# Attention values product in 64x32 array tiles instead of 32x32, with the weight quarters swapped by six SBUF transfers per block

## The chip, the cores and the metric

The kernel runs on one core of one Trainium2 chip. The metric is the device time of one execution in microseconds (us), the median of several runs. Five engines work beside each other: PE (TensorE, with PEld for its weight loads), DVE (VectorE), ACT (ScalarE), POOL (GpSimd) and SP (SyncE). Here SP computes nothing: it issues nearly all the transfers (DMAs), one after the other, in the order of the program, and when one of them must wait, all the later ones wait behind it.

## What is computed

A cross attention block with adaptive layer norm, all in 32-bit floats. The parts that matter:

```python
xq  = _ada_ln(x_q, t_vec, Wss_q, bss_q)        # x_q: (16, 1024, 512)
xkv = _ada_ln(x_kv, t_vec, Wss_kv, bss_kv)     # x_kv: (16, 64, 512)
q  = (xq @ Wq + bq).reshape(B, Lq, 16, 32)
kv = (xkv @ Wkv + bkv).reshape(B, 64, 2, 16, 32)
k, v = kv[:, :, 0], kv[:, :, 1]
scores = jnp.einsum('bqhd,bkhd->bhqk', q, k) / jnp.sqrt(32.0)
attn = jax.nn.softmax(scores, axis=-1)
out = jnp.einsum('bhqk,bkhd->bqhd', attn, v).reshape(B, Lq, 512)
return x_q + (out @ Wp + bp)
```

There are 16 heads of 32 features, and 64 keys to a batch.

## The kernel before

The 16 x 1024 query rows are cut into 32 blocks of 512 rows, numbered i; two blocks share the keys and values of one batch. The 512 features are 4 chunks c of 128, and each chunk holds 4 heads r. The 64 keys are 2 halves z of 32 keys.

The schedule is written out by hand: the order of the calls in the program is the order on every engine's queue. Blocks 0 to 2 are interleaved with the start (weights, keys, values), the loop over `i` from 3 to 29 (line 1404) has one block of each stage in flight, and the last two blocks are again written out. In one turn of the loop, block i is scored, block a = i-1 is mixed with the values, blocks b = i-2 and a are projected, block n = i+1 gets its queries, and the features of block f = i+2 are scaled.

The stages that the change and the prediction touch:

- `score_products` (651): for each half z, 16 matmuls with 32x32 tiles. The scores of head (c, r) lie on partitions 32c to 32c+31 (the 32 keys of the half) in column group r. So `s_tiles[i, z]`, 128 partitions x 4 heads x 512 queries, has the four chunks above one another and one half of the keys.
- `subtract` (715, POOL) takes the maxima `mb` off; `weights` (721, ACT) takes the exponential in place; `total` (753, POOL) adds the two halves; `row_total` (760, DVE) sums it over the keys.
- `inverse_rows` (774): DVE takes the reciprocal `lt`, and SP sends it to DRAM (`ltd`, one transfer) and back in another layout (`vr`, four transfers that wait until `ltd` has landed).
- `mix` (810): for each half z, chunk c and head r one matmul of a 32x32 tile over 512 queries: 32 in all, the second half added to the first in PSUM. `v_tiles` come from `V_all`, with the keys of a half on 32 partitions for each chunk.
- `value_move` (626): the values, computed with 128 keys of two batches on the partitions (`stages`), are moved into `V_all` by 8 transfers a call, in runs of 512 bytes; there are two calls for each of the two groups of batches, all near the start.
- `move` (381): the features of block i+3 change their layout by 16 transfers of 64 KB from SBUF to SBUF (`xt<-ht`); `scale_features` (444, ACT) waits for all 16 one turn later.
- `load_x` (106) loads 1 MB for block i+5; `load_residual` (122) loads 1 MB for block i into the buffer from which block b was just written out (`added`, 964, two transfers of 512 KB).

SP's order in one turn of the loop is: the two outputs, `load_residual`, `load_x`, `ltd`, four `vr`, sixteen `xt<-ht`. ACT's order around the weights is: first half's exponential (1435), `query_out`, `scale_features` of two chunks (1437), second half's exponential (1446).

Of the kernel before, what the change touches and what calls it, by code (L numbers as in the profile page):

```python
# [9 lines left out]
F32 = mybir.dt.float32  # L10
AF = mybir.ActivationFunctionType
ALU = mybir.AluOpType
# [3 lines left out]
P = 128  # L16
# [4 lines left out]
def cross_attention_block(  # L21
# [18 lines left out]
    nc = tc.nc  # L40
# [298 lines left out]
    def hidden(i, ts):  # L339

        for t in ts:
            row, rstd = x_tiles[i][:, t, :], q_rstd[i]
            if i == "A" and t % 2 == 0:
                nc.vector.tensor_scalar(
                    row, row, rstd[:, 0, t : t + 1], rstd[:, 1, t : t + 1], ALU.mult, ALU.add
                )
            else:
                normalise(row, row, rstd, t)
# [95 lines left out]
    def scale_features(i, cs=range(NC)):  # L444
        xt, b = xt_tiles[i], i // BPB
        for c in cs:
            nc.scalar.activation(  # L447
                xt[:, :, c, :],
                xt[:, :, c, :],
                AF.Identity,  # L450
                scale=ss["q"][:, c, b : b + 1],
                bias=ss["q"][:, NC + c, b : b + 1],
            )
# [25 lines left out]
    def feature_sums(i, eng=nc.gpsimd, steps=range(4)):  # L479

        if i in GROUPS:
            if i not in xsums:
                pool, tag = (big, "big1") if i == "A" else (opool, "ot")
                xsums[i] = pool.tile([P, 4, HC, HT], F32, tag=tag, name=f"xk_sums_{i}")
        else:
            if "q" not in xsums:
                xsums["q"] = qpool.tile([P, 4, 2, HC, P], F32, tag="wq", name="xt_sums")
            xsums[i] = xsums["q"]
        t = xsums[i]
        b12 = feature_half(i, 0, 1)  # L490
        for k in steps:
            dst, a, b = (
                (t[:, 0], feature_half(i, 1, 1), b12),
                (b12, b12, feature_half(i, 0, 0)),
                (t[:, 1], feature_half(i, 1, 1), b12),
                (t[:, 2], feature_half(i, 1, 0), t[:, 1]),
            )[k]
            eng.tensor_tensor(dst, a, b, ALU.subtract)  # L498
# [57 lines left out]
    def query_product(i, n):  # L556
        seven(i, "q", n, (0, 1))
# [27 lines left out]
            nc.vector.tensor_tensor(dst, src, dst, ALU.add)  # L585

    K_all = {g: kvpool.tile([P, NC, TB], F32, tag=f"K{g}", name=f"K_{g}") for g in GROUPS}
    V_all = {g: kvpool.tile([P, PER, 2, P], F32, tag=f"V{g}", name=f"V_{g}") for g in GROUPS}
    for g, at in GROUPS.items():
        for bl in range(PER):  # L590
            k_tiles[at * PER + bl] = K_all[g][:, :, bl * LKV : (bl + 1) * LKV]
            v_tiles[at * PER + bl] = V_all[g][:, bl]

    def key_out(i, n):
        k, m, h = OUTS[n]
# [12 lines left out]

    def value_places(i, m, h, k):
        if i not in stages:  # L610
            stages[i] = wpool.tile([P, NT, H], F32, tag="WT", name=f"stage_{i}")
        dst = stages[i][:, 2 * h : 2 * h + 2, m * HO : (m + 1) * HO]
        return qa["v", k].rearrange("p (t f) -> p t f", t=2), dst

    def value_out(i, n):
        k, m, h = OUTS[n]
        src, dst = value_places(i, m, h, k)
        b = b_v_sb[:, m * HO : (m + 1) * HO]
        nc.vector.tensor_tensor(dst, src, b.unsqueeze(1).to_broadcast([P, 2, HO]), ALU.add)

    def value_added(i, n):
        k, m, h = ADDS[n]
# [1 line left out]
        nc.vector.tensor_tensor(dst, src, dst, ALU.add)  # L624

    def value_move(i, m):
        for c in (2 * m, 2 * m + 1):
            for j in range(2):
                for z in range(2):
                    at = j * LKV + z * HK  # L630
                    nc.sync.dma_start(  # L631
                        V_all[i][32 * c : 32 * c + 32, j::2, z, :],
                        stages[i][at : at + HK, :, c * P : (c + 1) * P],
                    )

    def context_product(i, name, n):
        seven(i, name, n, CONTEXT_BANKS[i, name])
# [80 lines left out]

    l_tiles = {}

    def weights(i, z):
        p = s_tiles[i, z]
        nc.scalar.activation(p, p, AF.Exp, scale=SCALE)  # L723

    def sums(i, z):
        if z == 0:
            l_tiles[i] = small.tile([P, 2, HPC, NJ], F32, tag="l2", name=f"l2_{i}", bufs=1)
        nc.vector.tensor_reduce(
            l_tiles[i][:, z],
            s_tiles[i, z].rearrange("p r (j a) -> p r j a", a=32),  # L730
            AX.X,
            ALU.add,
            apply_transpose=True,
        )
# [18 lines left out]
    def total(i):  # L753

        pool, tag = (xpool, "x") if i == NB - 2 else (big, f"big{(i + 1) % 2 * 2}")
        t = pool.tile([P, HPC, TB], F32, tag=tag, name=f"sum_{i}")
        nc.gpsimd.tensor_tensor(t, s_tiles[i, 0], s_tiles[i, 1], ALU.add)  # L757
        sum_tiles[i] = t

    def row_total(i):  # L760
# [49 lines left out]
    def mix(i, apart=True, ks=(None,) * NC):  # L810

        vt = v_tiles[i // BPB]

        if apart:
            pairs = [ps_s.tile([P, 2, TB], F32, tag="s", name=f"po_{i}_{e}") for e in range(2)]
            po = [pairs[c // 2][:, c % 2, :] for c in range(NC)]
            po_tiles[i] = pairs
        else:
            po = [bank(f"po_{i}_{c}", ks[c]) for c in range(NC)]
            po_tiles[i] = po  # L820
        for z in range(2):
            p = s_tiles.pop((i, z))
            for c in range(NC):
                rows = slice(32 * c, 32 * c + 32)
                for r in range(HPC):
                    nc.tensor.matmul(  # L826
                        po[c][32 * r : 32 * r + 32, :],
                        lhsT=vt[rows, z, 32 * r : 32 * r + 32],
                        rhs=p[rows, r, :],
                        start=(z == 0),  # L830
                        stop=(z == 1),
                    )

    def mixed(i, es=(0, 1)):
# [389 lines left out]
    weights(0, 0)  # L1224
    turn(3, (0,))
    weights(0, 1)
    scale_features(2, (1,))
    total(0)
    hidden(3, (2,))
    q_stats(4, (2,))  # L1230
    query_product(1, 5)
# [61 lines left out]
    scale_features(3, (2,))  # L1293
    turn(4, (0,))
    weights(1, 1)
    feature_sums(2, nc.gpsimd, (3,))
    query_product(2, 7)
    query_product(2, 5)
# [6 lines left out]
    project_seeded(0, 0)  # L1305
    turn(4, (2,))
    total(1)
    query_added(2, 5)
    projected(0, 0)
    query_product(2, 4)  # L1310
# [57 lines left out]
    row_sums(1, 0)  # L1368
    turn(5, (0,))
    weights(2, 1)  # L1370
    scale_features(4, (1,))
    turn(5, (1,))
    added(1, 1)
# [6 lines left out]
    product(1, 2)  # L1380
    added(1, 2)
    total(2)
    query_product(3, 4)
    turn(5, (3,))
    biased(1, 3)
# [18 lines left out]
    for i in range(3, NB - 2):  # L1404
        a, b, n, f = i - 1, i - 2, i + 1, i + 2

        scores(i, 0, crossed=True)
        product(b, 6)
        added(b, 6)
        query_product(n, 1)  # L1410
        query_seed(n)
        added(b, 7)
        scores(i, 1)
        product(b, 5)
        added(b, 5)
        maxima(i)
        subtract(i)
        product(b, 4)
        if i < NB - 3:
            hidden(i + 3, (0, 1, 2))  # L1420
        query_product(n, 2)
        query_out(n, 2)
        product(b, 3)
        spread_rows(a)
        if i < NB - 3:
            hidden(i + 3, (3,))
        added(b, 4)
        added(b, 3)
        biased(a, 2)
        load_residual(i)  # L1430
        mix(a)
        divided(a)
        row_sums(a, 0)
        query_product(n, 6)
        weights(i, 0)
        query_out(n, 6)
        scale_features(f, (0, 1))
        product(a, 1)
        if i + 4 < NB:
            q_stats(i + 4, (0,))  # L1440
        added(a, 1)
        product(a, 2)
        if i + 4 < NB:
            q_stats(i + 4, (1,))
        added(a, 2)
        weights(i, 1)
        total(i)
        query_product(n, 7)
        query_out(n, 7)
        biased(a, 3)  # L1450
        scale_features(f, (2, 3))
        row_sums(a, 1)
        if i < NB - 3:
            turn(i + 3, range(NT))
        if i < NB - 5:
            load_x(i + 5)
        elif i == NB - 3:
            load_residual(NB - 1)
        query_product(n, 5)
        query_added(n, 5)  # L1460
        if i + 4 < NB:
            q_stats(i + 4, (2,))
        query_product(n, 4)
        query_added(n, 4)
        if i + 4 < NB:
            q_stats(i + 4, (3,))
        query_product(n, 3)
        query_out(n, 3)
        feature_sums(f)
        product(a, 7)  # L1470
        row_total(i)
        inverse_rows(i)
        if i + 3 < NB:
            move(i + 3)
        if i + 4 < NB:
            q_scale(i + 4)
# [28 lines left out]
    query_product(z, 3)  # L1505
    query_out(z, 3)
    weights(y, 1)
    total(y)
    product(y - 2, 3)
    added(y - 2, 3)  # L1510
    load_residual(y)
# [22 lines left out]
    product(y, 1)  # L1534
    added(y, 1)
    weights(z, 1)
    product(y, 2)
    added(y, 2)
    biased(z, 3)
# [73 lines left out]
```

## Time and profile before

| | |
|---|---|
| three runs | 1031.79, 1030.08, 1030.09 us (median 1030.09) |
| profiled execution | 1030.86 us, of which 1029.1 us are the span of the profile |
| PE busy | 1009.3 us of the span |
| POOL, DVE, ACT busy | 805.9, 860.9, 638.6 us |
| DMA | 149.82 MB, mean 146 GB/s; the engines' queue of SP 45.3% of the span |
| 500 to 529 us, one turn of the loop | PE busy 29.00 us of 29.00, granted clock 1.00, DMA share 0.47 |

"Busy" is the time in which an engine had an instruction running. A turn of the loop takes 29.1 us. The transfers that SP issues are not busy time of an engine; they are seen in SP's timeline (when each was issued) and in the share of the DMA engines.

### The profile page before, as it was taken

What the parts mean: (1) busy time and instruction counts of PE and PEld (TensorE: products, weight loads), DVE (VectorE), ACT (ScalarE), POOL (GpSimd) and SP (SyncE); (2) the same over time, 40 slices, a digit from 0 to 9 for tenths busy, and PEclk for the clock granted to TensorE, in tenths of its full rate; (3) what the DMA queues carried; (4) which work ended last, traced back from release to release, by engine and by line L of the source; (5) the groups of instructions that cost most, each with busy time, mean ns of one, the idle gap of its engine ahead of it and who ended that gap; (6) DMA issues with size and microseconds to landing.
All of it is one profiled execution on the core that took longest, in us unless ns stands there. A gap on an engine that the chain in (4) does not pass through costs nothing.

```text
span 1029.1 us, 21212 instructions
## 1 busy us (share of the span) xinstructions
PE 1009.3 (98%) x8077; PEld 763.4 (74%) x8077; DVE 860.9 (84%) x1174; ACT 638.6 (62%) x1025; POOL 805.9 (78%) x518
## 2 busy tenths in 40 slices
PE   8999899999999999999999999999999999999998
PEld 7877556777777777777777778777777777777746
DVE  6686669889888888889898888898888888876795
ACT  3786565666666666667666666666666676665530
POOL 4566687798888888898888888988888888987861
PEclk9999999999999999999999999999999999999999
DMA  9563544444544444445444444445434444335122
GB/s 318 179 188 119 149 122 136 157 157 156 165 155 121 143 128 154 152 152 166 140 134 146 150 133 153 156 159 165 148 110 151 134 154 154 113 125 166 46 85 85
DMA packets 112197, 149.82 MB, mean 146 GB/s; under 512 B 34104, under 2 KB 45392, under 8 KB 112096
## 3 DMA queue, kind: packets, MB, share of 16 engines
q1 hardware_dynamic: 111712, 147.94, 45.3%
q8 instruction: 64, 1.05, 0.4%
q0 software_dynamic: 384, 0.54, 0.3%
q14 instruction: 37, 0.30, 0.1%
HBM read 79.21 MB, written 34.60 MB: 111 GB/s over the span
## 4 chain that ended last, share of the span: by engine, by line
PE 81%; SPq 6%; DMA 5%; DVE 4%; ACT 1%; issue 1%; POOL 1%; DVEq 0%; ACTq 0%; POOLq 0%
PE pp L955 34%; PE pq L539 33%; PE po L826 6%; PE ps L658 6%; SPq L387 4%; DMA ltd<-lt 1%; SPq L631 1%; PE pk_A L539 1%; PE pv_A L539 1%; DMA xt<-ht 1%; DMA r<-in_x_dram 1%; DVE ht L365 1%; DVE lt L762 1%; DMA wss_kv<-in_L_xcond_Wss_kv_dram 1%; DMA x<-in_x_dram 1%
## 5 line engine op out<-in xcount | busy, mean ns | idle before, releaser
L717 POOL TENSOR_TENSOR s<-s,mb 128x2048 f32<-128x2048 f32 x64 | 290.2, 4558 | 129.3 <-DVE mb L704 127.7
L684 ACT COPY s<-ps 128x1024 f32<-128x1024 f32 x128 | 129.4, 1012 | 108.1 <-DVE m L675 64.8
L675 DVE TRANSPOSE_TENSOR_REDUCE m<-ps 128x32 f32<-128x1024 f32 x128 | 150.7, 1213 | 33.6 <-PE ps L658 33.4
L955 PE MATMUL pp<-w_p_sb,ot 128*128 128x256 f32 x720 | 165.6, 379 | 0.5 <-DVE r L979 0.4
L979 DVE TENSOR_TENSOR r<-pp,r 128x512 f32<-128x512 f32 x203 | 131.8, 670 | 30.9 <-PE pp L955 24.3
L578 ACT ACTIVATE qt<-pq,bias_t 128x256 f32<-128x256 f32 x256 | 105.6, 463 | 77.2 <-PE pq L539 77.0
L955 PEld LDWEIGHTS pp<-w_p_sb,ot 128*128 128x128 f32 x720 | 136.6, 190 | 20.5 <-issue 1.6
L723 ACT ACTIVATE s<-s 128x2048 f32<-128x2048 f32 x64 | 122.3, 1911 | 43.8 <-POOL s L717 43.8
L757 POOL TENSOR_TENSOR sum<-s,s 128x2048 f32<-128x2048 f32 x31 | 140.7, 4540 | 7.0 <-ACT s L723 7.0
L955 PEld LDWEIGHTS pp<-WT,s 128*128 128x128 f32 x480 | 86.5, 189 | 57.0 <-issue 37.7
L539 PE MATMUL pq<-xt_sums,w_q_sums 128*128 128x256 f32 x512 | 123.3, 385 | 0.0
L539 PE MATMUL pq<-xt,w_q_sums 128*128 128x256 f32 x512 | 121.1, 379 | 1.6 <-DVE qt L585 1.6
L539 PE MATMUL pq<-xt,w_q_sb 128*128 128x256 f32 x512 | 121.6, 380 | 0.3 <-ACT pq L551 0.2
L539 PEld LDWEIGHTS pq<-xt_sums,w_q_sums 128*128 128x128 f32 x512 | 94.9, 190 | 36.5 <-issue 24.8
L955 PE MATMUL pp<-WT,s 128*128 128x256 f32 x480 | 119.3, 391 | 0.2 <-POOL s L934 0.2
L955 PE MATMUL pp<-WT,ot 128*128 128x256 f32 x480 | 113.6, 379 | 0.6 <-POOL ot L931 0.6
L539 PEld LDWEIGHTS pq<-xt,w_q_sb 128*128 128x128 f32 x512 | 96.8, 190 | 16.4 <-issue 1.7
L539 PEld LDWEIGHTS pq<-xt,w_q_sums 128*128 128x128 f32 x512 | 97.2, 190 | 15.2 <-DVE qt L585 2.0
L955 PEld LDWEIGHTS pp<-WT,ot 128*128 128x128 f32 x480 | 91.0, 190 | 14.1 <-POOL ot L931 1.0
L335 ACT ACTIVATE x<-x,rstdq 128x512 f32<-128x512 f32 x128 | 97.0, 807 | 4.4 <-POOL rstdq L312 4.4
L447 ACT ACTIVATE xt<-xt,ss_q 128x512 f32<-128x512 f32 x124 | 93.9, 808 | 5.1 <-DMA xt<-ht 4.5
L498 POOL TENSOR_TENSOR xt_sums<-xt 128x512 f32<-128x512 f32 x64 | 81.4, 1272 | 14.2 <-ACT xt L447 7.3
(176 smaller groups left out, 1509.8 us busy)
## 6 DMA issues: line engine op xcount, KB each, us to landing
x<-in_x_dram SPq DMA_DIRECT2D x32, 1024.0 KB, 5.5
r<-in_x_dram SPq DMA_DIRECT2D x32, 1024.0 KB, 5.1
xt<-ht SPq DMA_DIRECT2D x488, 64.0 KB, 2.0
out_dram<-r SPq DMA_DIRECT2D x58, 512.0 KB, 3.7
out_dram<-r SPq DMA_DIRECT2D x11, 256.0 KB, 2.2
wss_kv<-in_L_xcond_Wss_kv_dram SPq DMA_DIRECT2D x4, 512.0 KB, 7.3
wss_q<-in_L_xcond_Wss_q_dram SPq DMA_DIRECT2D x4, 512.0 KB, 11.0
vr<-ltd SPq DMA_DIRECT2D x128, 8.0 KB, 1.6
```

Of the source, the lines that this page charges most:

```text
L335: nc.scalar.activation(dst, src, AF.Identity, bias=rstd[:, 1, j : j + 1], scale=rstd[:, 0, j : j + 1])
L447: nc.scalar.activation(xt[:, :, c, :], xt[:, :, c, :], AF.Identity, scale=ss["q"][:, c, b : b + 1], bias=ss["q"][:, NC + c, b : b + 1],)
L498: eng.tensor_tensor(dst, a, b, ALU.subtract)
L539: nc.tensor.matmul(out_, lhsT=lhsT, rhs=rhs, start=new and m == 0 and c == 0, stop=c == HC - 1, skip_group_check=True,)
L578: nc.scalar.activation(dst, src, AF.Identity, bias=bq_t[:, o : o + 1])
L675: nc.vector.tensor_reduce(m_tiles[i][:, z, 2 * e : 2 * e + 2, :], s_banks[i, z][e].rearrange("p r (j a) -> p r j a", a=32), AX.X, ALU.max, ...
L684: nc.scalar.copy(s_tiles[i, z][:, 2 * e : 2 * e + 2, :], s_banks[i, z][e])
L717: eng.tensor_tensor(s_tiles[i, z], s_tiles[i, z], mb_tiles[i], ALU.subtract)
L723: nc.scalar.activation(p, p, AF.Exp, scale=SCALE)
L757: nc.gpsimd.tensor_tensor(t, s_tiles[i, 0], s_tiles[i, 1], ALU.add)
L955: nc.tensor.matmul(acc[k][:, t * HO : (t + 1) * HO], lhsT=rows[:, c, t * P : (t + 1) * P], rhs=cols[:, c, :], start=n == 2 and t == 0 and ...
L979: nc.vector.tensor_add(r, a, r)
```

## The change

The product with the values works on array tiles of 64 rows and 32 columns: all 64 keys of a head lie on 64 adjacent partitions, and one matmul sums over all of them, so 16 matmuls a block stand where there were 32, and nothing is added in PSUM. For that the weights of the two halves must lie below each other. Of the four chunks, two lie right in each tile and a quarter (32 partitions, 256 KB) of each of the others is in the other tile, so quarters are swapped between the two tiles by transfers from SBUF to SBUF. The second half's exponential goes to a tile of its own (`p_`, in the buffer `spread` that the maxima `mb` also use), so that its old place can take the first half's quarters; four transfers fill that place (`paired(i, 1)`, after the exponential) and two fill the first tile (`paired(i, 0)`, called after `total`, which still reads the old contents). The values' tile gets the keys of a batch on 64 partitions, and `value_move` takes 2 transfers a call instead of 8, in runs of 4 KB.

```diff
-    V_all = {g: kvpool.tile([P, PER, 2, P], F32, tag=f"V{g}", name=f"V_{g}") for g in GROUPS}
+    V_all = {g: kvpool.tile([P, 2, 2, NT, P], F32, tag=f"V{g}", name=f"V_{g}") for g in GROUPS}
...
-            v_tiles[at * PER + bl] = V_all[g][:, bl]
+            v_tiles[at * PER + bl] = V_all[g][:, bl % 2, :, bl // 2, :]
...
     def value_move(i, m):
-        for c in (2 * m, 2 * m + 1):
-            for j in range(2):
-                for z in range(2):
-                    at = j * LKV + z * HK
-                    nc.sync.dma_start(
-                        V_all[i][32 * c : 32 * c + 32, j::2, z, :],
-                        stages[i][at : at + HK, :, c * P : (c + 1) * P],
-                    )
+        for j in range(2):
+            nc.sync.dma_start(
+                V_all[i][m * LKV : (m + 1) * LKV, j],
+                stages[i][j * LKV : (j + 1) * LKV, 2 * m : 2 * m + 2],
+            )
...
+    p_tiles = {}
+
     def weights(i, z):
-        p = s_tiles[i, z]
-        nc.scalar.activation(p, p, AF.Exp, scale=SCALE)
+        s = p = s_tiles[i, z]
+        if z == 1:
+            p = rpool.tile([P, HPC * TB], F32, tag="spread", name=f"p_{i}")
+            p = p.rearrange("p (r q) -> p r q", r=HPC)
+        nc.scalar.activation(p, s, AF.Exp, scale=SCALE)
+        p_tiles[i, z] = p
+
+    def paired(i, w):
+
+        for u in range(2):
+            first = slice(u * LKV, u * LKV + HK)
+            second = slice(u * LKV + HK, (u + 1) * LKV)
+            if w == 1:
+                nc.sync.dma_start(s_tiles[i, 1][first], p_tiles[i, 0][second])
+                nc.sync.dma_start(s_tiles[i, 1][second], p_tiles[i, 1][second])
+            else:
+                nc.sync.dma_start(s_tiles[i, 0][second], p_tiles[i, 1][first])
...
-        nc.gpsimd.tensor_tensor(t, s_tiles[i, 0], s_tiles[i, 1], ALU.add)
+        nc.gpsimd.tensor_tensor(t, p_tiles[i, 0], p_tiles[i, 1], ALU.add)
...
-        for z in range(2):
-            p = s_tiles.pop((i, z))
-            for c in range(NC):
-                rows = slice(32 * c, 32 * c + 32)
+        for w in (1, 0):
+            p = s_tiles.pop((i, w))
+            for u in range(2):
+                rows = slice(LKV * u, LKV * (u + 1))
                 for r in range(HPC):
                     nc.tensor.matmul(
-                        po[c][32 * r : 32 * r + 32, :],
-                        lhsT=vt[rows, z, 32 * r : 32 * r + 32],
+                        po[2 * u + w][32 * r : 32 * r + 32, :],
+                        lhsT=vt[rows, w, 32 * r : 32 * r + 32],
                         rhs=p[rows, r, :],
-                        start=(z == 0),
-                        stop=(z == 1),
+                        start=True,
+                        stop=True,
                     )
...
         weights(i, 1)
+        paired(i, 1)
         total(i)
+        paired(i, 0)
         query_product(n, 7)
```

The last hunk is the loop's; blocks 0 to 2, 30 and 31 get the two calls too, the last of them without `total`. On SP's queue the six transfers of the loop come behind `load_residual(i)` and before `load_x(i + 5)`. The stage of the values (`value_places`, `value_out`) is written in the new layout with the same number of instructions.

More of the change, by code (lines that the diff above doesn't have):

```diff
@@ L610, in value_places @@
         if i not in stages:
-            stages[i] = wpool.tile([P, NT, H], F32, tag="WT", name=f"stage_{i}")
-        dst = stages[i][:, 2 * h : 2 * h + 2, m * HO : (m + 1) * HO]
-        return qa["v", k].rearrange("p (t f) -> p t f", t=2), dst
+            stages[i] = wpool.tile([P, NC, NT, P], F32, tag="WT", name=f"stage_{i}")
+        dst = stages[i][:, 2 * m : 2 * m + 2, 2 * h : 2 * h + 2, :]
+        return qa["v", k].rearrange("p (t c f) -> p c t f", t=2, c=2), dst
     def value_out(i, n):
@@ L617, in value_out @@
         src, dst = value_places(i, m, h, k)
-        b = b_v_sb[:, m * HO : (m + 1) * HO]
-        nc.vector.tensor_tensor(dst, src, b.unsqueeze(1).to_broadcast([P, 2, HO]), ALU.add)
+        b = b_v_sb[:, m * HO : (m + 1) * HO].rearrange("p (c f) -> p c f", c=2)
+        nc.vector.tensor_tensor(dst, src, b.unsqueeze(2).to_broadcast([P, 2, 2, P]), ALU.add)
     def value_added(i, n):
@@ L729, in sums @@
             l_tiles[i][:, z],
-            s_tiles[i, z].rearrange("p r (j a) -> p r j a", a=32),
+            p_tiles[i, z].rearrange("p r (j a) -> p r j a", a=32),
             AX.X,
@@ L1226, in cross_attention_block @@
     weights(0, 1)
+    paired(0, 1)
     scale_features(2, (1,))
     total(0)
+    paired(0, 0)
     hidden(3, (2,))
@@ L1295, in cross_attention_block @@
     weights(1, 1)
+    paired(1, 1)
     feature_sums(2, nc.gpsimd, (3,))
@@ L1307, in cross_attention_block @@
     total(1)
+    paired(1, 0)
     query_added(2, 5)
@@ L1370, in cross_attention_block @@
     weights(2, 1)
+    paired(2, 1)
     scale_features(4, (1,))
@@ L1382, in cross_attention_block @@
     total(2)
+    paired(2, 0)
     query_product(3, 4)
@@ L1507, in cross_attention_block @@
     weights(y, 1)
+    paired(y, 1)
     total(y)
+    paired(y, 0)
     product(y - 2, 3)
@@ L1536, in cross_attention_block @@
     weights(z, 1)
+    paired(z, 1)
+    paired(z, 0)
     product(y, 2)
```

## The prediction

> **What bounds the kernel now.** I first read the page's busy times and the granted clock, then one turn of the loop on each engine's timeline (500 to 532 us), then SP's, since six transfers a block are added there. PE is busy for 98% of the span, and for all 29.00 us of the window 500 to 529 at a clock of 1.00: in the loop PE sets the pace, 29.1 us a turn.
>
> ```profile
> PE 1009.3 (98%) x8077; PEld 763.4 (74%) x8077; DVE 860.9 (84%) x1174; ACT 638.6 (62%) x1025; POOL 805.9 (78%) x518
> ```
>
> The product with the values on PE's timeline (start, length, then the group):
>
> ```profile
> 514.87 1.14 PE L658 MATMUL ps<-qt,K_A 32*32 32x512 f32 x32
> 515.94 1.99 PE L955 MATMUL pp<-WT,s 128*128 128x256 f32 x8
> ...
> 527.77 2.35 PE L826 MATMUL po<-s,V_A 32*32 32x512 f32 x64
> 530.04 1.13 PE L539 MATMUL pq<-xt_sums,w_q_sums 128*128 128x256 f32 x4
> ```
>
> From start to next start the product takes 530.04 - 527.77 = 2.27 us. A matmul of the program shows as two records, so 64 records are 32 matmuls. Taken record by record, sixteen start within 0.1 us at 527.77, the next sixteen at 528.22, then at 528.84 and at 529.29: the sixteen 32x32 tiles truly run together, in four waves of about 0.43 us (512 columns), 1.72 us, and 0.55 us go into starting, the step between the halves (528.65 to 528.84) and the end.
>
> Now SP's timeline of one turn:
>
> ```profile
> 499.56 2.49 SPq L387 DMA_DIRECT2D xt<-ht  x4
> 502.15 1.07 SPq L981 DMA_DIRECT2D out_dram<-r  x2
> 508.34 0.38 SPq L126 DMA_DIRECT2D r<-in_x_dram  x1
> 509.50 0.38 SPq L119 DMA_DIRECT2D x<-in_x_dram  x1
> 516.66 0.34 SPq L780 DMA_DIRECT2D ltd<-lt  x1
> 518.17 1.75 SPq L782 DMA_DIRECT2D vr<-ltd  x4
> 520.03 10.80 SPq L387 DMA_DIRECT2D xt<-ht  x16
> 530.92 1.07 SPq L981 DMA_DIRECT2D out_dram<-r  x2
> ```
>
> SP is one chain with few holes. It waits 508.34 - 503.22 = 5.1 us until the output has landed before the residual can be loaded into its buffer, then for the features' buffer (509.5), then 6.8 us for `lt` (516.64), then 1.2 us until `ltd` has landed, then 16 features' transfers every 0.635 us. Whatever is later than `lt` on SP makes the features later, and these have little room: the last leaves at 530.83 and, at the 2.0 us from issue to landing that the page gives for `xt<-ht`, lands at 532.3, and ACT scales them at 504.65 + 29.1 = 533.75. The room is 1.4 us. On ACT, POOL and DVE:
>
> ```profile
> 504.65 1.51 ACT L447 ACTIVATE xt<-xt,ss_q 128x512 f32<-128x512 f32 x2
> 506.63 1.91 ACT L723 ACTIVATE s<-s 128x2048 f32<-128x2048 f32 x1 [0.47 <-POOL s L717]
> ```
> ```profile
> 509.16 4.54 POOL L757 TENSOR_TENSOR sum<-s,s 128x2048 f32<-128x2048 f32 x1
> ```
> ```profile
> 513.74 2.31 DVE L762 TRANSPOSE_TENSOR_REDUCE lt<-sum 128x64 f32<-128x2048 f32 x1 [0.64 <-POOL sum L757]
> 516.09 0.55 DVE L777 RECIPROCAL lt<-lt 128x64 f32<-128x64 f32 x1
> ```
>
> Behind the scaling on ACT stand the second exponential, the next `query_out` and the seeds of PE's banks, so a late feature soon stops PE.
>
> **The matmuls.** 16 matmuls are 32 records. No 64-row tile is in the trace. Eight such tiles fill the array, so 32 records are again four waves of 512 columns: 1.72 us. What may go is part of the 0.55 us: the score product (one call of 32 records) has 515.94 - 514.87 = 1.07 us for two waves, 0.21 us over. I take 1.72 + 0.21 = 1.93, a gain of 0.34 us a block; the ends are no gain and 0.55. At 32 blocks that is 11 us, between 0 and 18, and only if PE goes on setting the pace. (The Trainium skill, TensorEngine Tiling (Array Packing), section Tiling Modes, lists 64x32 as a mode of 8 tiles; no run here shows it yet.)
>
> **The exponential, total, sums and values** keep their count and sizes, so cost nothing more. `spread` is now held by `p_` until the last swap has landed, where `mb` of the next block is written at 523.97 (its transpose on DVE); that is 15.4 us behind the exponential's end at 508.54, and the swap ends some 13 us behind it by the sum below, so it fits with 2 us. `mix` comes 19.2 us behind. `value_move` loses 24 of its 32 issues at 0.64 us, 15 us of SP's time between 62 and 134 us.
>
> **The six transfers.** Their issues are 6 x 0.62 = 3.7 us, less than SP's holes. What counts is where they stand: behind the residual's load and before `load_x`, `ltd`, `vr` and `move`, on one queue. The first four wait for the exponential (508.54), the fifth for `total` (513.70) and the first's landing, the sixth for the third's landing; `load_x` then leaves behind the sixth instead of at 509.5, and `ltd` behind both. Transfers of one queue land in order; that shows where `load_x` stands just before `ltd` already (chain of waits, 135 us): `ltd` then takes 5.16 us from its issue instead of 1.5 (516.66 to 518.17).
>
> ```profile
> 134.96 0.40 SPq L119
> 135.35 0.05 issue
> 135.41 5.16 DMA ltd<-lt
> ```
>
> The speed of a 32-partition transfer from SBUF to SBUF is read where the DMA engines are full. The windows view gives span, busy times, clock, DMA share, GB/s:
>
> ```profile
> 77.20:79.20 2.00, 2.00 (x11) 1.77 (x10) 1.97 (x2) 1.11 (x4) 0.95 (x1) 1.00 1.03 392
> 79.80:81.00 1.20, 1.20 (x7) 1.07 (x6) 0.00 (x0) 1.20 (x3) 1.20 (x1) 1.00 1.09 219
> ```
>
> The first is a load from HBM, the second mostly eight queued `xt<-ht`. So a quarter of 256 KB takes 262/219 = 1.20 us; at the load's rate it would be 0.67.
>
> The chain on SP, from `ltd` landed to the residual's issue, by the timeline: vr 1.77, to the first xt 0.1, 16 x 0.635 = 10.16, two outputs with gaps 1.1, their landing 5.1, the issue 0.4: 18.6 us. Then from that issue's end: the residual's 1 MB keep the DMA engines full until about 512.6 (share 0.96 in 510.0 to 512.5, 0.67 after), which is +3.9. The four quarters end at +5.1, 6.3, 7.5, 8.7. The third has landed at +7.8, so the sixth issue ends at +8.4, `load_x` at +8.85, `ltd` at +9.2. Quarters five and six end at +9.9 and +11.1, `load_x` (1 MB at 392 GB/s, 2.7) at +13.8, and `ltd` has landed at +14.1. The turn of this chain is 18.6 + 14.1 = 32.7 us, more than PE's 29.1: SP's queue sets the pace, 3.6 us more a turn, and PE's 0.34 us buys nothing.
>
> Sum against the profiled execution (1030.86): 24 turns (3 to 26) x 3.6 = 86. Turns 27 and 28 have no `load_x`: 32.7 - 3.1 = 29.6, 1 us in two. Blocks 0 to 2: `load_x` or the residual stood before `ltd` already, SP saves issues of values, but 7.2 us of quarters are queued in each, of which waits for loads hide most; I take +4 (-5 to 10). The end: the last exponential ends at 1000.47 and `ltd` left at 1003.75; six quarters on an idle queue (3.7 us of issues, 1.2 and 1.4 for the sixth) land at about 1008, `vr` then at 1011 instead of 1008, +3. The room of 1.4 comes off. 86 + 1 + 4 + 3 - 1.4 = 93: 1124 for an execution like the profiled one; the median of before was 0.8 lower, so **1123**.
>
> Bounds of a quarter: 0.67 us by the load's row gives landings of the third at +6.2, `load_x` issued at +7.25 and, with its own 1.3 us to the first data, done at +11.2, `ltd` +11.5: 30.1 us, 24 + 6 = 30 more, 1060. From above: the 512-byte rows of `V_B<-stage_B` took about half the rate of `xt<-ht` where the queue was full; but rows of 8 KB are nearer to the 2 KB rows. Half way, 1.6 us, gives 18.6 + 16.5 = 35.1 and 150 us more, 1180.
>
> A rule speaks against this change and yet is kinder than the row. The Trainium skill, DMA: Bandwidth & Descriptors, section Rules for kernel authors, says that transfers to separate parts of the partitions serialize, since each is spread over all 16 engines, and its Specifications give 435 GB/s as the ceiling. At that rate a quarter would be 0.60 us, the turn about 30, and an estimate from this page some 1057. The row (219 GB/s) decides.
>
> **Rivals.** (1) The swap is quick: the same chain at the load's rate, 30.1 us a turn, 1060. For it: 8 KB runs are longer than any in this trace; against: the 219 GB/s. Chance 0.20. (2) Not slower: the swap is hidden. It decides on one place, `ltd`'s landing: while that is less than 1.4 us later than now, the features are in time and PE keeps the pace. SP has 6.8 us free before `ltd`, and quarters 3.7 us of issues; if `load_x` moved 1 MB in the time before `lt`, only the matmuls' gain would be left: 1030 - 0.34 x 32 = 1019. Against it: the sixth quarter waits for the third, at about `lt`. 0.10. (3) The 64x32 tiles run one after the other: 32 x 0.43 = 13.8 us a block instead of 2.3, 368 us more, 1398. Against it: sixteen small tiles run together here. 0.03. The forecast has 0.67.
>
> **How the numbers follow.** The range 1050 to 1170 holds the forecast with most of its bounds, and rival 1. This kernel's measurement tells about 0.2% from no change. Faster is most of rival 2: 0.08; same the rest of it and a chain just at 29.1: 0.03; slower 0.89.
>
> **What would show it.** In the profile after: PE's share falls to about 90%, the chain of waits runs through SP (lines of the swap, `ltd`, `xt<-ht`, the outputs) in the loop, `ltd` takes over 4 us to land in each turn, ACT's scaling (now line 447 too) waits for `xt<-ht`, and a turn takes 32 to 33 us. The product's group would show 32 records in some 1.9 us. I am wrong if the quarters land together at over 350 GB/s, if `load_x` is not delayed to the sixth quarter, or if PE's turn stays at 29 us.

## The result, and the profile after

| | before, on the same chip | changed kernel |
|---|---|---|
| median | 1030.94 us (4 runs, 1030.08 to 1036.01) | 1202.3 us (4 runs, 1193.21 to 1204.45) |
| ratio | | 1.163 [1.156, 1.171] |
| profiled execution, its span | 1030.86, 1029.1 us | 1201.12, 1199.3 us |
| one turn of the loop, mean of blocks 3 to 26 | 29.1 us | 35.2 us |

The change costs 171 us, where 93 were forecast. The page's first part, busy time and share of the span for each engine:

```profile
PE 1049.7 (88%) x7053; PEld 779.5 (65%) x7053; DVE 866.4 (72%) x1174; ACT 637.2 (53%) x1025; POOL 805.3 (67%) x518
```

PE has 1024 records fewer than before, the 16 matmuls a block that went, and yet it is no longer the bound: 88% of a span that is 170 us longer. The product on PE's timeline of the changed kernel (start, length, group):

```profile
570.02 1.95 PE L840 MATMUL po<-s,V_A 64*32 64x512 f32 x32
571.89 1.35 PE L539 MATMUL pq<-xt_sums,w_q_sums 128*128 128x256 f32 x5
```

From start to next start it takes 571.89 - 570.02 = 1.87 us; before it took 2.27. The matmuls do what they should. The time is lost on SP. Its timeline of one turn, to be held against the one of before:

```profile
571.19 10.02 SPq L387 DMA_DIRECT2D xt<-ht  x16
581.31 1.06 SPq L995 DMA_DIRECT2D out_dram<-r  x2
585.71 0.38 SPq L126 DMA_DIRECT2D r<-in_x_dram  x1
586.18 0.51 SPq L734 DMA_DIRECT2D s<-s  x1
586.74 0.58 SPq L735 DMA_DIRECT2D s<-p  x1
587.38 0.59 SPq L734 DMA_DIRECT2D s<-s  x1
588.01 0.59 SPq L735 DMA_DIRECT2D s<-p  x1
595.27 2.62 SPq L737 DMA_DIRECT2D s<-p  x2
597.93 0.58 SPq L119 DMA_DIRECT2D x<-in_x_dram  x1
598.61 0.67 SPq L794 DMA_DIRECT2D ltd<-lt  x1
604.15 2.19 SPq L796 DMA_DIRECT2D vr<-ltd  x4
```

Four quarters go out behind the residual's load. The fifth (595.27) waits until the first has landed and the sixth until the third has; only then do `load_x` (line 119) and `ltd` (794) leave. `ltd` lands 5.5 us later, and the 16 features' transfers, 10 us of issues, stand behind it. The chain of waits joins the same pieces (start, length, what):

```profile
580.62 2.00 DMA xt<-ht
...
582.76 1.52 ACT xt L447 x2
584.28 1.80 ACT p L725
...
587.38 9.98 DMA s<-s
...
598.61 5.52 DMA ltd<-lt
```

In this turn it closes on itself: the features land late, ACT scales them late, the second exponential stands behind the scaling, the quarters wait for the exponential, `ltd` waits for the quarters, and the next features wait for `ltd`. Not every turn's chain looks like this. Followed through blocks 3 to 26, it passes through `ltd` in 11 turns and through the swap in 3 (blocks 8, 14 and 17); in most of the others it runs from the exponential through PE's matmuls to the next features, whose issue then waited for PE by 0.7 us at most. So a second road is nearly as long as the one through the swap; that the swap started it all is shown by the run without transfers below. In the general view of waits the scaling's line (us in total, times, longest) shows how often the late features are felt:

```profile
ACT xt L447 <- DMA xt<-ht: 107.3, 29, 5.0
```

Two views show what the transfers themselves do. First the residual's load in the page's issues (KB each, median us to landing), of the changed kernel:

```profile
r<-in_x_dram SPq DMA_DIRECT2D x32, 1024.0 KB, 7.0
```

and of the kernel before:

```profile
r<-in_x_dram SPq DMA_DIRECT2D x32, 1024.0 KB, 5.1
```

The load, ahead of the quarters on its queue, lands 1.9 us later than it did (medians). Then the windows view (span, the engines' busy times, clock, DMA share, GB/s): the first 2.4 us behind the residual's issue, the bulk of its data, and a stretch of quarters; and below the first 2.4 us in the kernel before:

```profile
586.10:588.50 2.40, 1.55 (x7) 1.43 (x8) 1.57 (x4) 2.40 (x5) 2.34 (x1) 1.00 0.54 59
588.50:591.00 2.50, 2.50 (x13) 2.19 (x13) 1.82 (x5) 0.56 (x2) 2.50 (x2) 1.00 0.98 337
591.50:595.00 3.50, 3.50 (x45) 2.10 (x44) 3.46 (x4) 2.22 (x8) 3.34 (x4) 1.00 1.06 228
```

```profile
508.72:511.12 2.40, 2.40 (x13) 2.10 (x12) 1.97 (x5) 2.40 (x5) 2.40 (x2) 1.00 0.52 179
```

At the same DMA share the load moved 59 GB/s in place of 179 at its start; over the loop's turns the medians are 87 and 185. All 69 packets that start in the changed kernel's 2.4 us are smaller than the quarters' rows of 8 KB, so the quarters' data aren't moving yet. The quarters run at 228 GB/s, which is 262 KB / 228 = 1.15 us each, near the forecast's 1.20.

### The profile page after: what moved, and what is told of

It reads as the page before. It is cut to its first block, busy times and chain, and to the rows that moved or that the text cites. A ratio compares the mean times of both kernels' runs of the same rounds, so it can differ in the third digit from the quotient of the medians.

```text
span 1199.3 us, 19452 instructions
## 1 busy us (share of the span) xinstructions
PE 1049.7 (88%) x7053; PEld 779.5 (65%) x7053; DVE 866.4 (72%) x1174; ACT 637.2 (53%) x1025; POOL 805.3 (67%) x518
## 2 busy tenths in 40 slices
DMA packets 117439, 200.05 MB, mean 167 GB/s; under 512 B 36792, under 2 KB 43984, under 8 KB 111200
## 4 chain that ended last, share of the span: by engine, by line
PE 32%; SPq 20%; DMA 18%; DVE 8%; ACT 8%; issue 7%; POOL 6%; ACTq 0%; DVEq 0%; POOLq 0%
SPq L387 16%; PE pp L969 12%; PE pq L539 12%; DMA ltd<-lt 7%; DMA s<-s 4%; POOL s L714 3%; PE ps L655 3%; DMA xt<-ht 3%; ACT p L725 3%; POOL sum L771 3%; ACT xt L447 3%; SPq L796 2%; DVE m L672 2%; DVE lt L776 1%; ACT qt L578 1%
## 5 line engine op out<-in xcount | busy, mean ns | idle before, releaser
L969 PE MATMUL pp<-w_p_sb,ot 128*128 128x256 f32 x720 | 202.0, 440 | 88.8 <-DVE ot L820 85.7
L969 PEld LDWEIGHTS pp<-w_p_sb,ot 128*128 128x128 f32 x720 | 158.7, 224 | 127.1 <-ACT pp L932 79.6
L771 POOL TENSOR_TENSOR sum<-s,p 128x2048 f32<-128x2048 f32 x31 | 140.6, 4534 | 149.8 <-ACT p L725 143.6
L672 DVE TRANSPOSE_TENSOR_REDUCE m<-ps 128x32 f32<-128x1024 f32 x128 | 153.3, 1228 | 36.8 <-PE ps L655 36.6
L802 DVE STREAM_TRANSPOSE vb<-vr 128x2048 f32<-128x2048 f32 x32 | 73.9, 2309 | 106.5 <-DMA vr<-ltd 106.5
L539 PE MATMUL pq<-xt_sums,w_q_sb 128*128 128x256 f32 x256 | 68.6, 416 | 46.3 <-ACT qt L578 46.2
```

Of the source, the lines that this page charges most:

```text
L539: nc.tensor.matmul(out_, lhsT=lhsT, rhs=rhs, start=new and m == 0 and c == 0, stop=c == HC - 1, skip_group_check=True,)
L672: nc.vector.tensor_reduce(m_tiles[i][:, z, 2 * e : 2 * e + 2, :], s_banks[i, z][e].rearrange("p r (j a) -> p r j a", a=32), AX.X, ALU.max, ...
L771: nc.gpsimd.tensor_tensor(t, p_tiles[i, 0], p_tiles[i, 1], ALU.add)
L802: nc.vector.transpose(t.rearrange("p c q -> p (c q)"), v.unsqueeze(2).to_broadcast([P, NC * NJ, 32]))
L969: nc.tensor.matmul(acc[k][:, t * HO : (t + 1) * HO], lhsT=rows[:, c, t * P : (t + 1) * P], rhs=cols[:, c, :], start=n == 2 and t == 0 and ...
```

## The experiments

Theory A was the place: the six transfers stand on the path from the exponential through `ltd` to the features, and their cost is what they make `ltd` and the features wait. Theory B was the volume: 1.5 MB more a block through DMA engines that are busy already, wherever they are queued. Rival C was that something else of the change (tiles, the layout of the values, the new buffer) costs. Kernels with an interval were timed in several runs; the others are one execution each, which is enough for differences of 40 us and more. Beside these runs the kernel before took 1032.6 to 1033.6 (medians).

**The whole change without its transfers.** `paired` issues nothing, so the weights aren't swapped.

```diff
-        for u in range(2):
+        for u in range(0):
```

> The changed kernel without its six transfers a block: the 64x32 product, the values' layout and the second half's exponential into a tile of its own stay, the weights are not swapped (the product gets wrong rows). Theory A (the transfers' place on SP's queue makes the loss): PE sets the pace again and only the product's gain is left, 1030.9 - 32 x 0.40 (the product takes 1.87 us from start to next start in the changed kernel's profile, against 2.27) = 1018, and up to 8 less if the shorter move of the values helps the start; 1008 to 1025. Rival C (the product in 64x32 tiles, or the buffer of the maxima that is now held longer, makes part of it): clearly above 1031.

Measured 1018.14 us, 0.986 [0.984, 0.988] of before; PE is back at 98% of the span. Without its transfers the change gains 14 us. A turn takes 28.78 us in place of 29.10, so 0.32 us of it is gained a block in the loop (7.6 us in 24 turns); 3.5 us are there by block 2, before the loop; whether the shorter `value_move` gives them was not split. All the loss, 1202 - 1018 = 184 us, comes with the six transfers. Rival C falls, but for one part that this run doesn't try, as no swap holds the buffer of the maxima here. The changed kernel's own trace answers that: in all 32 blocks `mb` follows the instruction before it on DVE within 0.04 us, and wherever a swap goes before, it starts at least 0.4 us behind the last quarter's landing, so it never waited for the buffer.

**Four of them, and two of them.**

```diff
-        for u in range(2):
+        for u in range(2 if w == 1 else 0):    # four only
+        for u in range(2 if w == 0 else 0):    # two only
```

> Only the four transfers that follow the exponential; the two that wait for the total and for the third's landing are left out (one tile of the product then holds wrong rows). Theory A, by the changed kernel's own times: load_x leaves right behind the fourth, at +3 us from the residual's issue instead of +12; residual, four quarters and load_x are 5.2 + 4.8 + 2.7 = 12.7 us of data, so ltd lands at about +13 instead of +18: a turn of 30.1 us instead of 35.1, about 1060. Rival B (the volume counts, in any order: 1.5 MB a block cost 171 us): two thirds of the volume are left, so two thirds of the loss, 1030 + 114 = 1145.

> Only the two transfers behind the total; the four before are left out (wrong rows again). Theory A: there is no third to wait for; the two leave when the total has ended, load_x about 1.2 us behind, ltd when lt is there, and it lands some 6 us behind load_x: a turn of about 29.4 to 30, 1035 to 1060; and four alone plus two alone cost far less than the six together. Rival B: a third of the loss, 1030 + 57 = 1087, and the two parts add up to the whole.

Measured 1110.67 and 1090.54 us, 92 and 72 over the kernel without transfers; together 165 of the 184. Four lie midway between A and B (1060 and 1145) and settle nothing. That two transfers cost nearly as much as four speaks for a wait. SP's timeline with two only:

```profile
601.59 1.15 SPq L737 DMA_DIRECT2D s<-p  x2
602.83 0.55 SPq L119 DMA_DIRECT2D x<-in_x_dram  x1
605.75 0.35 SPq L794 DMA_DIRECT2D ltd<-lt  x1
610.36 1.75 SPq L796 DMA_DIRECT2D vr<-ltd  x4
```

The two now hold `load_x` back until 602.83, 3 us ahead of `ltd` (7 us in the kernel before), which so has 1 MB in front of it and lands 4.6 us after its issue. The load of the residual lands in 5.5 us here, and in 6.9 with the four directly behind it. But A as expected priced this far too low (1035 to 1060), and B's figure (1087) was hit: at this point the two theories were not told apart.

**`load_x` behind `ltd`, with the two.** The same transfers, one of them in another place.

```diff
-        if i < NB - 5:
-            load_x(i + 5)
...
         row_total(i)
-        inverse_rows(i)
+        inverse_rows(i, lambda: later_load(i))   # load_x between ltd and vr
```

> As the run with only the two transfers behind the total (one tile of the product holds wrong rows), with load_x behind ltd instead of before, in the loop. Theory A: the cost of those two was that load_x, put behind the total by them, stood before ltd: with it behind, ltd lands some 1.5 us from its issue and the turn is PE's again, 1018 to 1035. Rival B: the same two transfers, so again 1085 to 1095.

Measured 1038.38 us, 52 less with the same bytes, 3 above A's range and far below B's. SP's timeline:

```profile
606.53 1.15 SPq L737 DMA_DIRECT2D s<-p  x2
609.47 0.35 SPq L794 DMA_DIRECT2D ltd<-lt  x1
609.87 0.43 SPq L119 DMA_DIRECT2D x<-in_x_dram  x1
610.99 1.74 SPq L798 DMA_DIRECT2D vr<-ltd  x4
```

`ltd` lands 1.5 us after its issue. So of the 72 us that two transfers cost, 52 were the place of a load that they had pushed in front of `ltd`; volume alone is at most the other 20.

**The two behind `ltd`, then `load_x` too, with all six.**

```diff
-        paired(i, 0)
...
-        inverse_rows(i)
+        inverse_rows(i, lambda: paired(i, 0))                    # first
+        inverse_rows(i, lambda: (paired(i, 0), later_load(i)))   # second
```

> All six transfers, the same bytes, and the full computation; in the loop the last two stand between ltd and vr instead of before load_x. Theory A: load_x and ltd no longer wait for the third quarter's landing; ltd lands at about +13 instead of +18 from the residual's issue, the two fill the wait for it, but the sixth still waits for the third at +11 and is issued by +12: a turn of 30 to 32 us, 1060 to 1110. Rival B: same volume, so no change, 1195 to 1205.

> The full computation, all six transfers. As the run with the last two between ltd and vr, and load_x behind them as well; the residual's load stays before the quarters. Theory A: before ltd stand the residual and four quarters, 5.1 to 6.5 us and 4.8 us from the residual's issue, so ltd lands at +11.5, against +14 where load_x stood before it too; vr behind it: a turn of 29 to 31, 1030 to 1080. Rival B: 1155 to 1165, as that run.

Measured 1159.6 and 1108.14 us: 43 and then again 51 less, neither as much as A asked; B, which asked for no change, missed both times. In the first, `ltd` lands 7.2 us (median) after its issue, behind a `load_x` that now leaves directly behind the four quarters. In the second it takes 4.4 us, behind the quarters themselves, and the fourth of the features' transfers, with which `load_x` shares no data, waits for `load_x` to land (613.97 to 620.60 on the chain of waits). Each move bought something and made the next transfer late.

**Another queue.** All six issued by ACT, the two at a place where ACT is free; then also `load_x` behind `ltd`.

```diff
-                nc.sync.dma_start(s_tiles[i, 1][first], p_tiles[i, 0][second])
+                nc.scalar.dma_start(s_tiles[i, 1][first], p_tiles[i, 0][second])
```

> All six transfers and the full computation, but issued by ACT on its own queue: four behind the seeds of PE's second bank, two in the next turn between the two halves' score copies. SP's queue is as in the kernel before. Theory A: the turn falls back to near PE's, 28.7 to 30 us; ACT has 10 us idle a turn for 3.7 us of issues; loads are slowed by sharing the DMA engines: 1015 to 1060. Rival B (volume): 1150 to 1205, as the same 1.5 MB a block pass through the same DMA engines.

> As the run on ACT's queue, and in the loop load_x stands behind ltd and vr instead of before. Theory A: ltd no longer lands behind load_x, whose data now share the DMA engines with the quarters; 0 to 1 us a turn less than that run, 1012 to 1040, perhaps below the kernel before. Rival B: no different from that run.

Measured 1345.81 and 1311.75 us, 1.302 [1.299, 1.305] and 1.271 [1.267, 1.274]: misses, far the wrong way. ACT's timeline of the first:

```profile
629.03 1.35 ACTq L737 DMA_DIRECT2D s<-p  x2
630.42 1.93 ACT L681 COPY s<-ps 128x1024 f32<-128x1024 f32 x2 [11.20 <-DMA xt<-ht]
```

and its waits (us in total, times, longest):

```profile
ACT s L681 <- DMA xt<-ht: 284.5, 27, 12.0
```

ACT stands 11 us at the issue of the two, released by transfers of the features, with which they share no data. The semaphore events of the traces have eight counters of finished transfers, handed out in rotation in the program's order, so that a transfer can stand and wait for an earlier one with the same counter, on whatever queue that is; with SP's queue alone it is always the eighth before it. The traces bear it out. In this run none of 997 transfers from SP and ACT went out before the last one on its counter had landed. The two here leave at 629.03 and 629.66, and the features' transfers on their counters had landed at 629.01 and 629.64; 54 of ACT's issues leave so, within 0.1 us of such a landing. No run gave the transfers other counters, so what this wait costs in us is not shown. The two runs say what a wait on a computing engine's queue costs, and nothing of volume.

**The order on SP: four quarters, residual, two quarters, `ltd`, `load_x`.**

```diff
         biased(a, 2)
-        load_residual(i)
         mix(a)
...
         paired(i, 1)
+        load_residual(i)
         total(i)
         paired(i, 0)
...
-        inverse_rows(i)
+        inverse_rows(i, lambda: later_load(i))
```

> The full computation, all six transfers, the same bytes, all on SP's queue; only the order on it differs, in the loop and for blocks 0 to 2: four quarters behind the exponential, then the residual's load, the two last quarters, ltd, load_x, vr, the features. No load stands before the quarters, and none but the residual's before ltd. Theory A (what stands before ltd on the queue): quarters leave at 508.6 to 511 of the kernel before's turn, the fifth and sixth behind the total at 513.8, ltd at 516.7 and lands at 518.2 to 519.5; the features land within their room or 1 us late: PE's turn of 28.8 to 29.8, 1018 to 1045. Rival B (the volume of 1.5 MB a block, on any place): 1150 to 1200.

Measured 1153.27 us, 1.116 [1.114, 1.118]: a miss. The residual between the quarters lands in 10.2 us (median), and `ltd` behind it in 7.8. The wait had only been handed on.

**Both loads among the features' transfers**, so that only quarters stand ahead of `ltd`.

```diff
-            move(i + 3)
+            loads = {9: lambda: load_residual(i), 3: lambda: load_x(i + 5)}
+            move(i + 3, loads=loads)
```

> The full computation, all six transfers on SP's queue, the same bytes; in the loop both 1 MB loads stand between the features' transfers (load_x behind the second, the residual behind the eighth), so that only the six quarters stand before ltd; blocks 0 to 2 have load_x behind ltd. Theory A, now with the runs so far (load_x before ltd costs 52 us, the sixth's wait before it 42, the residual and four quarters the rest): the chain ltd, vr 1.9, features with two loads and one wait 12.1, landing 1.5, scaling and exponential 3.4, total 4.6, lt 2.9, ltd 1.8 is 28.2 us, just under PE's 28.7: 1018 to 1040. If the volume has a share of its own (rival B, kept as a rest: loads and features share the DMA engines), the features land late and the turn is 29.5 to 31: 1040 to 1085.

Measured 1126.03 us, 1.088 [1.085, 1.091]: a miss. `ltd` now takes 2.5 us (median), but the features have 2 MB in between, and some of their issues wait until a load has landed; 53 of them leave within 0.1 us of the landing of a load, the eighth transfer before them (for these counters see the two runs on ACT's queue). The waits of SP:

```profile
SPq L388 <- DMA r<-in_x_dram: 50.5, 23, 3.3
...
SPq L388 <- DMA x<-in_x_dram: 42.4, 28, 3.4
```

**Half of the features ahead of the wait for `ltd`.** They need nothing of this block, so they can fill SP's wait for the quarters: four quarters, four features, two quarters, `ltd`, four features, `vr`, three features, `load_x`, five features, the outputs, the residual.

```diff
+        some(0, 4)
+        paired(i, 0)
         feature_sums(f)
         product(a, 7)
         row_total(i)
-        inverse_rows(i)
-        if i + 3 < NB:
-            move(i + 3)
+        inverse_rows(i, lambda: some(4, 8))
+        some(8, 11)
+        if i < NB - 5:
+            load_x(i + 5)
...
+        some(11, 16)
```

> The full computation, all six transfers on SP's queue, the same bytes. In the loop the features' transfers no longer stand behind ltd and vr, on which they do not depend: four quarters, four features, two quarters, ltd, four features, vr, three features, load_x, five features, outputs, residual. Blocks 0 to 2 have load_x behind ltd. Theory A (the turn is the sum of what stands in one line: features' transfers, their landing, scaling, exponential, quarters, total, lt, ltd, vr, and again the features' transfers): the line is cut at ltd, since a late ltd no longer makes the features late; SP's own work in a turn is 18 us, the features land some 4 us before they are needed, PE sets the pace again: 28.7 to 29.5 a turn, 1018 to 1040. Rival B (the volume of the quarters slows the loads and features wherever they stand): not below 1108, the best of the full versions with the loads late.

Measured 1059.23 us, 1.025 [1.023, 1.028]: 143 us less than the changed kernel with the same six transfers and the same bytes (in both, 200.05 MB moved by the page). SP's timeline:

```profile
580.24 0.51 SPq L736 DMA_DIRECT2D s<-s  x1
...
584.29 3.56 SPq L387 DMA_DIRECT2D xt<-ht  x4
587.95 2.90 SPq L739 DMA_DIRECT2D s<-p  x2
590.89 0.59 SPq L796 DMA_DIRECT2D ltd<-lt  x1
591.53 0.65 SPq L387 DMA_DIRECT2D xt<-ht  x1
```

and its longest sum of waits:

```profile
SPq L126 <- DMA out_dram<-r: 149.0, 31, 6.5
```

Eight of the features' 16 transfers now leave before SP waits for `ltd` (by `vr`), a turn is about 30.1 us, and 143 of the 184 us are back: they were place, and the rival that the volume alone keeps the time above 1108 falls. A asked for more, 1018 to 1040. The other 41 over the kernel without transfers were not split further. Part can be the volume (the features take 3.9 us to land, 2.0 before), part can be a wait that this order still has, the residual's load behind the landing of the outputs (102.7 us in all in the kernel before, where no quarters stood behind it).

**The same with the residual behind the four quarters.**

```diff
         biased(a, 2)
-        load_residual(i)
         mix(a)
...
         paired(i, 1)
+        load_residual(i)
         total(i)
```

> The full computation, as the run with the features before ltd, but in the loop the residual's load stands behind the four quarters instead of before them, and for blocks 2 and 30 it stands behind ltd. Theory A: the quarters no longer wait for the outputs' landing and the residual's 2.7 to 4 us of data, so the sixth and ltd leave 2 to 3 us earlier; the residual's data then stand before the sixth and ltd instead; the turn falls from 30.0 to 29 to 29.8 and the end by 3 to 5 us: 1035 to 1056, against 1059. Rival B (what is left is the volume): the same bytes in another order, 1057 to 1066. That it falls below the kernel before is not expected: without any transfer the product gains 14 us, and the turn has less room than the quarters' data.

Measured 1105.05 us, 1.069 [1.067, 1.071]: a miss again. SP's waits show the new ones:

```profile
SPq L387 <- DMA r<-in_x_dram: 82.1, 27, 4.1
SPq L736 <- DMA x<-in_x_dram: 40.9, 24, 2.1
```

The features, which the load had just been put in front of, wait for its landing (the fifth is the eighth transfer behind it, with the load's counter). No version with the swap beat the kernel before; 1018 us, without the transfers, is the most that any of them could hope for.

## Why the prediction was right in kind and too low

**The matmuls** were right: 1.93 us forecast for the product, 1.87 measured; a gain of 0.34 us a block, 0.32 measured with the transfers gone. The 32 records start in four waves of eight (570.02, 570.47, 570.90 and 571.33), so eight 64x32 tiles run together and the rival of serial tiles falls.

**The mechanism** was right in the main. SP's queue took the place of PE as the bound, PE's gain bought nothing, `ltd` takes 5.6 us (median) to land, ACT's scaling waits for `xt<-ht`, PE's share fell to 88%. The chain runs through `ltd`, `xt<-ht` and at times the swap, but not through the outputs, which the forecast had on it: in the loop they are nowhere on the chain of waits. From the features' landing it goes through ACT's scaling and exponential to the first quarter, a road that the sum leaves out. It did no harm to the sum, for the two end together (the exponential at 586.08, the residual's issue behind the outputs at 586.09). The rate of a quarter was right: over the loop the four land 1.19 us apart (medians) against 1.20, so the rival with the load's rate falls, and so does the one in which the swap is hidden. The Trainium skill's ceiling (DMA: Bandwidth & Descriptors, Specifications) is 435 GB/s, from which the prediction estimated 0.60 us a quarter; the runs show about twice that, and the row of this kernel's own trace was the better guide.

**The length of the turn** was wrong: 32.7 us forecast, 35.2 measured. Its first term, from `ltd` landed to the residual's issue end, came out shorter, 17.07 us in the turn shown (569.02 to 586.09) against 18.6, as the outputs landed in 3.3 us and not 5.1. The second, from there to the next landing of `ltd`, was 18.04 and not 14.1. The step that failed is "The third has landed at +7.8, so the sixth issue ends at +8.4, `load_x` at +8.85, `ltd` at +9.2". Measured from the same point, the four quarters landed at +9.1, 10.1, 11.3 and 11.85 (the turn after: 7.9, 9.2, 10.3, 11.55) in place of 5.1, 6.3, 7.5 and 8.7, and the sixth's issue ended at +11.8. The spacing holds; the first of them is 3 to 4 us late (+8.0, 9.2, 10.5 and 11.55 are the medians of the loop). Two things were left out. The working started the quarters' row at the end of the bulk of the residual's data (+3.9), though the load's landing came later, and the first quarter doesn't land before that: the page's 5.1 us from the start of the issue are +4.7, and in the turn that was read it was +5.1. And the load was taken at its old pace, while it lands in 7.0 us with quarters right behind it: the run with only the four transfers shows 6.9, those with two or none 5.4 to 5.5. The first point, 0.8 to 1.2 us, was to be had from the trace of before; the second, 1.4 to 1.9 us, no row of before showed. Together they are 2.7 of the 2.9 us by which the median first quarter is late; in the turn shown it landed another 1.2 us behind the load, which stays open. Why the load is slower is open too.

Two side readings of the working are off, without consequence: seven, not eight, `xt<-ht` are queued in its window of 219 GB/s, and by its own sum the swap ends 11.3 us behind the exponential, not 13.

**The sum** then runs as follows. By `ltd`'s landings the changed kernel is behind the one before by 9.4 us at block 2, by 155.1 at block 26 and by 170.2 at the end of the span. So the start took 9.4 where 4 were allowed. The 24 turns took 145.7 (6.07 each) where 86 less the room of 1.4 were. The end took 15 where 4 were: turns 27 and 28, without `load_x`, are still 32.6 and 31.0 us long, and turn 29 is 34.85, for there the loop has a residual's load in the place of `load_x`, which the working passed over. Of the 77 us missing, 61 are the turn.

**The bound above** was reached by a wrong road: a quarter of 1.6 us gave 35.1 us a turn. It priced the rate of the swap, while the doubt belonged to the load ahead of it.

**Place or volume** was not priced apart in the prediction. It says that where the six stand is what counts, but costs them as so many bytes on that one line and tries no other place. The runs answer most of it: 52 us for moving `load_x` alone, with two transfers and again (51) with six, and 143 us for the order of the queue.

## What to carry to other kernels

A transfer that is added to a queue is priced by what then stands behind it and by who waits for that: here two transfers of 1.2 us cost 72 us, 52 of them because they left a 1 MB load just in front of a transfer of 32 KB for which the next features waited. Count to the landing of what stands ahead, not to the end of its data, and walk each variant of the loop's last turns. Where a queue's order closes a loop, moving one transfer mostly hands the wait on (five of the orders tried here did that); filling the wait with transfers that don't depend on what is waited for opened most of it, though no order made the change pay.

## What the runs showed of the hardware

- A load from HBM with SBUF-to-SBUF transfers directly behind it on the queue started at 59 GB/s in place of 179 over its first 2.4 us, with the DMA engines as busy (0.54 and 0.52), and landed in 7.0 us in place of 5.1 (medians). That the engines take rows of both in turn doesn't explain it, for none of the quarters' 8 KB rows starts in these 2.4 us. Nor do the quarters explain all of it: without any, one turn shows 139 GB/s there, at a share of 0.61, and the load lands in 5.5 us. The cause is open.
- The transfers of SP and ACT share eight counters of completion, and none left before the last one on its counter had landed (in none of six traces, with 829 to 997 transfers each).
- Transfers of SP's queue landed in the order of their issue in these kernels: all 837 before, all 1005 after.
- Rows of 8 KB moved hardly faster between SBUF and SBUF than the forecast's 219 GB/s for rows of 2 KB: 228 GB/s at a DMA share of 1.06.
- PE's mean granted clock was lower where PE stood idle more: 0.998 before (PE busy 98%), 0.997 without the transfers (98%), 0.96 in the changed kernel (88%), 0.917 in the slowest experiment (84%).
